# A two-layer graph network on one core: nine gathered slots a tile in place of ten, and three PSUM banks in turn

## The chip, the cores and the metric

The kernel runs on one core of a Trainium2 chip. The metric is the device time of one execution in microseconds (us). The core has five engines with a queue each: TensorE (PE, matrix products; PEld is its loading of weights), VectorE (DVE), ScalarE (ACT), GpSimd (POOL) and SyncE (SP, which issues transfers). Each executes its queue in order; they meet through semaphores. PSUM, into which PE writes, has eight banks of 128 x 512 f32.

## The reference

```
adj: 4096 x 4096, an entry off the diagonal with a chance of 0.00195, values 0.05 to 1; the diagonal always
layer 0:  a = adj + I;  d = rowsum(a) ** -0.5
          out = relu((d a d) @ x @ W.T + b);   h = layernorm(x + out)
layer 1:  the same form, attention of 8 heads over a mask: maximum(adj, I), and -1e16 * (1 - mask) on the scores
          h = layernorm(h + att @ v @ Wo)
```

Entries of `adj` lie below one, so in layer 1 an entry below one off the diagonal still gets a penalty of 1e15 or more; each node attends to itself alone, and the layer comes to one product with `Wv @ Wo`. The kernel tests that this holds (`test`), and has a general kernel behind a branch for the other case. What is left is layer 0, a sparse product: a row of `adj` has 8 edges on average, 21 at most.

## The kernel before

Rows are handled in 32 tiles of 128 (`NT`, `P`). There are two stages with a barrier between.

**First stage.** For each tile, `y = d * (x @ W.T)` is computed and written to DRAM: `x` is loaded, transposed on PE into a PSUM tile `pt` (`transpose_rows`), copied to `xT` by ACT (`evacuate`), multiplied (`times`), scaled by ACT with `d` (`keep_y`) and stored. `d` needs the row's sum, for which the whole tile of `adj` (2 MB) is loaded; ACT sums it (`sum_rows`). On the tiles in `early` and, in the second stage, on the others, DVE extracts the edges: eight segments of 512 columns, in each the eight largest values and their columns (MAX8, FIND_INDEX8), then short steps that sort a row's edges into 24 places of a record `rec` (`extraction`). These are 16 long steps a tile; `some` issues them in portions. Fifteen tiles (`again`) are loaded once more in the second stage (`reload`).

**Matching.** A row with more edges than there are slots passes its surplus to rows with few. `match` takes each tile through six steps: KEY (a key from the number of edges), ACROSS (PE transposes the key into `pk`), RANKS (how many keys are smaller: the row's rank), PERM (DVE compares the rank with `sources` and gets one 0/1 matrix per map), MOVE (PE multiplies the record by these matrices: lane l gets the row of rank l, and in its last slots the surplus of another row), END (DVE reads the moved fields into `wr_all` and `cols_all`). `KH` is 10: ten edges a lane. `ROUTES` has three maps (lane at which rank 0 goes, first and last place of the surplus). `SAME` is the number of slots that only hold a lane's own edges, 5. `pk` and the moved fields lie in one PSUM tile, `bank`; `pt` has two further banks, the sums `acc` five.

**Second stage, the gather loop.** Loop index `i` over the tiles in `order`, inner index `k` over the slots. For each slot POOL issues one indirect transfer of 128 rows of `y` (256 KB, `gather`, 18 slots ahead, 19 buffers), ACT builds the 128 x 128 matrix that puts the lanes' weights into their rows (`spread`: a square and a Relu for the slots from `SAME` on, one scaled copy for the others), and PE adds the product to `zs[i]` (L1265). The last two tiles (`SUMMED`) first add up the `SAME` slots on DVE (`presum`) and have six products (L1084). Behind the tile come `scaled` (L1126), `residual`, the transposes of `h`, the product with `wvo` and the second normalisation, at places that the function `at` sets. The steps of matching have places too:

```
match(*{1: (RANKS,), 3: (MOVE, PERM), 6: (END,), 7: (KEY,), 9: (ACROSS,)}.get(k, ()))
```

The order of instructions on each engine isn't quite that of the program: a planner with its own estimates of durations orders them and gives the PSUM and SBUF buffers, and an instruction waits where a buffer's last reader isn't done. The key's transpose and the first move are kept in program order.

Of the kernel before, what the change touches and what calls it, by code (L numbers as in the profile page):

```python
# [9 lines left out]
FP = mybir.dt.float32  # L10
# [4 lines left out]
P = 128  # L15
# [404 lines left out]
def few_edges_below_one(  # L420
# [18 lines left out]
    nc = tc.nc  # L439
    N, D = x.shape  # L440
    H, _, KD = wks.shape
    NT = N // P
# [7 lines left out]
    TS = SW // P  # L450
    C = SEGS * E
    K = 24
    KH = 10

    ROUTES = ((112, 10, 14), (120, 14, 19), (76, 19, 24))
    SAME = KH - max(hi - lo for _, lo, hi in ROUTES)

    const = ctx.enter_context(tc.tile_pool(name="const", bufs=1))
    small = ctx.enter_context(tc.tile_pool(name="small", bufs=4))
# [3 lines left out]
    keys = ctx.enter_context(tc.tile_pool(name="keys", bufs=2))  # L463
    dram = ctx.enter_context(tc.tile_pool(name="dram", bufs=1, space=bass.MemoryType.DRAM))
    mt = ctx.enter_context(tc.tile_pool(name="match", bufs=1))
    ps_t = ctx.enter_context(tc.tile_pool(name="ps_t", bufs=2, space=bass.MemoryType.PSUM))
    ps_a = ctx.enter_context(tc.tile_pool(name="ps_a", bufs=5, space=bass.MemoryType.PSUM))
    first = ExitStack()
    p1 = first.enter_context(tc.tile_pool(name="first", bufs=2))
# [22 lines left out]

    sources = const.tile([P, 1 + len(ROUTES), P], BF, name="sources")

    def ranks(dst, step, base):
        nc.gpsimd.iota(
            dst, pattern=[[step, dst.shape[1]]], base=base, channel_multiplier=0,
            allow_small_or_imprecise_dtypes=True,
        )

    ranks(sources[:, 0], 2, 1 - P)
    for n, (c, _, _) in enumerate(ROUTES):
        ranks(sources[:, n + 1, : c + 1], -2, 2 * c + 1 - P)
        ranks(sources[:, n + 1, c + 1 :], -2, P - 1)

    place = const.tile([P, 2, C], U32, name="place")
    for f, (per_seg, per_edge, base, shift) in enumerate(
# [16 lines left out]
    own_all = const.tile([P, NT], FP, name="own_all")  # L524
    cols_all = const.tile([P, NT, KH], U32, name="cols_all")

    wr_all = const.tile([P, NT, 4, KH], FP, name="wr_all")
    y = dram.tile([N, D], FP, name="y")
# [20 lines left out]
    order = early + resident + again  # L549
# [110 lines left out]
    def transpose_rows(src, dcs=range(ND)):  # L660
        pt = ps_t.tile([P, 512], FP, name="pt")
        for dc in dcs:
            nc.tensor.transpose(pt[:, ts(dc, P)], src[:, ts(dc, P)], ident)  # L663
        return pt
# [132 lines left out]
        return long, short  # L797


    bank = ps_t.tile([P, 512], FP, name="bank", bufs=1)  # L800
    second = []

    def match_key(t):
# [7 lines left out]
        return key  # L811

    def match_across(key):
        pk = bank[:, :P]
        tc.keep_in_program_order(nc.tensor.transpose(pk, key.to_broadcast([P, P]), ident))  # L815
        return pk

# [17 lines left out]
    def match_move(rec, perm):  # L835

        r = upper(rec)
        merged = bank[:, P : P + 7 * KH].rearrange("p (f k) -> p f k", f=7)
        tc.keep_in_program_order(
            nc.tensor.matmul(merged, perm[:, 0], r[:, :, :KH], start=True, stop=False)  # L840
        )
        for n, (_, lo, hi) in enumerate(ROUTES):
            nc.tensor.matmul(
                merged[:, :, KH - (hi - lo) :], perm[:, n + 1], r[:, :, hi - 1 : lo - 1 : -1],
                start=False, stop=(n == len(ROUTES) - 1),
            )
        return merged
# [15 lines left out]
    matched = set()  # L863
    begun, picked, sorted_ = [], [], []
    KEY, ACROSS, RANKS, PERM, MOVE, END = range(6)
# [73 lines left out]
    queue = list(again)  # L939
    reloaded, scanned = [], []  # L940
# [54 lines left out]
    for t in range(NT + 1):  # L995
# [8 lines left out]
        lo, hi = t + 1 + (t > EARLIER), t + 1 + (t >= EARLIER)  # L1004
        ahead = [j for at, j in due if lo <= at <= hi]
        pts = []
# [42 lines left out]
    SUMMED = (NT - 2, NT - 1)  # L1049
# [20 lines left out]
    def presum(i, k):  # L1070
        g = slots[i * KH]
        w = wr_all[:, order[i], 1, k : k + 1]
        if k == 0:
            nc.scalar.activation(g, g, AF.Copy, scale=w)
            return
        nc.vector.scalar_tensor_tensor(
            g, slots.pop(i * KH + k), w, g, op0=ALU.mult, op1=ALU.add
        )
# [52 lines left out]
    def residual(i, c=slice(0, D), part=0):  # L1131
        if i % 2 == 0 and i not in sts:
            sts[i] = small.tile([P, 2, 5], FP, name="sums")
            sts[i + 1] = sts[i][:, 1]
            pairs[i] = sts[i]
            sts[i] = sts[i][:, 0]
        nc.vector.scalar_tensor_tensor(
            hs[i][:, c], hs[i][:, c], 0.0, xs[i][:, c], op0=ALU.max, op1=ALU.add,
            accum_out=sts[i][:, part : part + 1],
        )  # L1140
# [65 lines left out]
    yo, zs, hs, pts, hTs, ws, sts, pairs, mats, halves = ({} for _ in range(10))  # L1206
# [24 lines left out]
    for i in range(NT + 2):  # L1231
        if i < NT:
            zs[i] = ps_a.tile([P, D], FP, name="acc")
        free = len([t for t in scanned if t in picked])
        p = i - 1
        has_p = 0 <= p < NT
        for k in range(KH):
            ends = p == NT - 1
            t = at("T", i, k)
            if t not in (None, NT - 1):  # L1240
                hTs[t] = evacuate(p2, "hT", transpose_rows(hs[t]))
            t = at("M", i, k)
            if t not in (None, NT - 1):
                ws[t] = times(hTs.pop(t), wvo)
            if i == NT - 1:

                if k <= KH - SAME:
                    summed_products(i, k, HALVES[0])
                if k == 7:
                    scaled(i, HALVES[0])  # L1250
                    residual(i, HALVES[0])
                if k == 8:
                    pts[i] = transpose_rows(hs[i], (0, 1))
                if k == 9:
                    for n in range(KH - SAME + 1):
                        summed_products(i, n, HALVES[1])
                    hTs[i] = p2.tile([P, ND, P], FP, name="hT", bufs=2)
                    nc.scalar.copy(
                        hTs[i][:, 0:2].rearrange("p c s -> p (c s)"), pts[i][:, : 2 * P]
                    )  # L1260
            elif i in SUMMED:
                if k <= KH - SAME:
                    summed_products(i, k)
            elif i < NT:
                nc.tensor.matmul(  # L1265
                    zs[i], mats[i][:, k, :], slots.pop(i * KH + k),
                    start=(k == 0), stop=(k == KH - 1),
                )
            if i < NT:
                gather(i * KH + k + AHEAD)  # L1270
            build(1)
            if i + 1 in SUMMED and k >= 5:
                presum(i + 1, k - 5)
            if k == 1 and has_p and not ends:
                scaled(p)
            some(next(shares, count[1]))
            if k == 1 and has_p and not ends:
                residual(p)
            if ends and k == 0:
                scaled(p, HALVES[1])  # L1280
                residual(p, HALVES[1], 4)
                ws[p] = times(hTs[p], wvo, dcs=(0, 1))
            if ends and k == 2:
                pts[p] = transpose_rows(hs[p], (2, 3))
                nc.scalar.copy(hTs[p][:, 2:].rearrange("p c s -> p (c s)"), pts[p][:, 2 * P : D])
                nc.vector.tensor_tensor(sts[p][:, 0:1], sts[p][:, 0:1], sts[p][:, 4:5], ALU.add)
            if ends and k == 3:
                times(hTs[p], wvo, ws[p], (2, 3))
            if k == 2:
                load_own(i + 2)  # L1290
            if k == 3 and i + 1 < NT:
                own_part(i + 1)
            t = at("Q", i, k)
            if t is not None:
                squares(ws[t], D**-0.5, sts[t][:, 3:4])

            t = at("V", i, k)
            if t is not None:
                variance(t)
                if t >= NT - 2:  # L1300
                    power(t, 1)
                elif t % 2:
                    power(t - 1, 2)
            if k == 6 and i < NT:
                own_bias(i)
            if k == 6 and has_p:
                eps_var(p)
            t = at("F", i, k)
            if t is not None and (t >= NT - 2 or t % 2):
                if t < NT - 2:  # L1310
                    finish(t - 1)
                finish(t)
            if k in (3, 9):
                scan_half()
            if staged[KEY] < NT - 2:
                match(*{1: (RANKS,), 3: (MOVE, PERM), 6: (END,), 7: (KEY,), 9: (ACROSS,)}.get(k, ()))
            elif k % 2:
                match(*ALL)
            if k == 9 and queue and len(reloaded) < free:
                reload()  # L1320
            while k == 1 and i + 2 < NT and order[i + 2] not in matched:
                some(count[0] + 1)
                match(*ALL)
        if i == NT - 7:
            su2 = load_keys()
        if i == NT - 4:
            square_sums(su2)
        if i == NT - 2:
            test()
# [25 lines left out]
```

## Time and profile before

| what | value |
|---|---|
| runs | 746.01, 750.56, 754.48 us; median 750.56 |
| profiled execution | span 744.8 us from first to last instruction; the page has no other time of it |
| PE, DVE, ACT, POOL busy | 591.2, 545.4, 525.2, 393.2 us |
| moved by DMA | 230.54 MB, 310 GB/s over the span |
| first gather | 221.85 us |
| first slot product (L1265) | 228.38 us |
| last output | ACT at 732.91 us |

A row of the page's groups has the line, the engine, the operation, its tiles and how often it stands there; then the busy time, the mean of one in ns, the idle time of the engine just before, and what ended most of it. A row of the timeline has the start and the length in us, and in brackets the idle time before it and who ended it. A program line belongs to the kernel before; the changed kernel's lines are up to nine further down.

### The profile page before, as it was taken

The numbers are of one execution on the slowest core, as the hardware profiler recorded it, in microseconds if no ns is written. First come the engines' busy times: TensorE is split into PE (matmuls) and PEld (weight loads), VectorE is DVE, ScalarE is ACT, GpSimd is POOL, SyncE is SP. The second block draws the span as 40 slices with busy tenths as digits, with TensorE's granted clock in tenths as the row PEclk, the third lists the DMA queues.
The fourth block names the chain that finished last, engine by engine and source line by source line (L and its number), as shares of the span: only waits on it lengthen the run. The fifth ranks groups of instructions, "written<-read, shape, count | busy, mean of one in ns | idle before, by whom it ended". The sixth has DMA issues, their size and how long they took to land. (4 is left out here: it accounts for less than half of the span.)

```text
span 744.8 us, 8023 instructions
## 1 busy us (share of the span) xinstructions
PE 591.2 (79%) x1638; PEld 273.9 (37%) x1638; DVE 545.4 (73%) x2109; ACT 525.2 (71%) x1152; POOL 393.2 (53%) x494
## 2 busy tenths in 40 slices
PE   1799959867815687989979699979996789898692
PEld 0444424433302233434434344434442334343350
DVE  6779899999997289889978799959994443322410
ACT  1787798958975287688958597867884887773432
POOL 3224233322337656766666666666665566667500
PEclk9999999999967778999999899999998899999896
DMA  8999999999947689999999988989996577777601
GB/s 341 403 422 426 425 423 406 421 430 413 423 187 262 198 294 366 343 371 373 380 305 343 325 300 313 337 297 333 351 333 209 171 221 239 224 240 248 199 24 62
DMA packets 54411, 230.54 MB, mean 310 GB/s; under 512 B 8592, under 2 KB 9616, under 8 KB 48080
## 3 DMA queue, kind: packets, MB, share of 16 engines
q0 software_dynamic: 30800, 100.95, 40.6%
q1 hardware_dynamic: 18416, 119.55, 40.5%
q10 hardware_dynamic: 5136, 9.44, 3.4%
q14 instruction: 44, 0.36, 0.1%
q8 instruction: 15, 0.25, 0.1%
HBM read 213.12 MB, written 16.78 MB: 309 GB/s over the span
## 5 line engine op out<-in xcount | busy, mean ns | idle before, releaser
L1057 POOL DMA_INDIRECT g<-y,cols_all x320 | 312.9, 978 | 151.0 <-issue 82.6
L1265 PE MATMUL acc<-g,s_t 128*128 128x512 f32 x600 | 283.6, 619 | 20.0 <-ACT s_t L959 20.0
L731 DVE MAX8 v_all<-a_t 128x8 f32<-128x512 f32 x256 | 168.8, 679 | 18.1 <-DMA a_t<-in_adj_dram 18.1
L732 DVE FIND_INDEX8 idx<-v_all,a_t 128x8 uint32<-128x512 f32 x256 | 174.0, 683 | 0.0
L1265 PEld LDWEIGHTS acc<-g,s_t 128*128 128x128 f32 x600 | 116.2, 200 | 151.9 <-issue 124.4
L675 PE MATMUL acc<-wvo,hT 128*128 128x512 f32 x256 | 125.4, 630 | 25.4 <-issue 14.8
L675 PE MATMUL acc<-wT,xT 128*128 128x512 f32 x256 | 121.7, 621 | 16.4 <-ACT xT L668 12.2
L687 ACT ACTIVATE dump<-a_t 128x2048 uint8<-128x2048 f32 (+1 forms) x52 | 119.5, 2297 | 0.0
L675 PEld LDWEIGHTS acc<-wvo,hT 128*128 128x128 f32 x256 | 49.1, 200 | 87.6 <-issue 71.9
L675 PEld LDWEIGHTS acc<-wT,xT 128*128 128x128 f32 x256 | 48.3, 198 | 72.3 <-issue 50.2
L955 ACT ACTIVATE sq<-cols,wr_all 128x128 f32<-128x128 f32 x192 | 66.9, 391 | 9.9 <-issue 7.3
L959 ACT ACTIVATE s_t<-sq,wr_all 128x128 f32<-128x128 f32 x160 | 72.0, 483 | 1.6 <-ACT sq L955 1.2
L968 ACT ACTIVATE s_t<-s_t,wr_all 128x128 f32<-128x128 f32 x150 | 52.4, 391 | 4.6 <-issue 3.8
L682 ACT ACTIVATE dump<-a_n 128x4096 uint8<-128x4096 f32 x15 | 54.5, 3632 | 0.3 <-DMA a_n<-in_adj_dram 0.3
L744 DVE MAX8 top<-key 128x8 f32<-128x64 f32 x192 | 39.0, 214 | 12.1 <-issue 7.3
L1119 DVE SCALAR_TENSOR_TENSOR yo<-yo,own_all,b_bc 128x512 f32<-128x512 f32 x32 | 23.8, 744 | 24.1 <-DMA yo<-y 10.4
L1126 DVE SCALAR_TENSOR_TENSOR h<-acc,d_all,yo 128x512 f32<-128x512 f32 (+1 forms) x33 | 23.9, 724 | 23.5 <-PE acc L1265 11.3
L540 POOL DMA_DIRECT2D x_t<-in_x_dram x32 | 17.9, 564 | 41.2 <-PE pt L663 41.0
L694 POOL TENSOR_SCALAR deg<-deg_all 128x1 f32<-128x1 f32 x32 | 6.7, 220 | 62.4 <-ACT dump L682 62.3
L704 POOL DMA_DIRECT2D y<-y_t x32 | 19.0, 593 | 38.6 <-ACT y_t L702 38.1
L702 ACT ACTIVATE y_t<-acc,d_all 128x512 f32<-128x512 f32 x32 | 21.6, 686 | 22.6 <-POOL d_all L697 16.7
L815 PE MATMUL bank<-ident,rank_key 128*128 128x128 f32 x32 | 10.2, 320 | 33.4 <-issue 11.5
(123 smaller groups left out, 651.5 us busy)
## 6 DMA issues: line engine op xcount, KB each, us to landing
a_t<-in_adj_dram SPq DMA_DIRECT2D x30, 2048.0 KB
a_n<-in_adj_dram SPq DMA_DIRECT2D x15, 2048.0 KB
x_t<-in_x_dram POOLq DMA_DIRECT2D x32, 256.0 KB
y<-y_t POOLq DMA_DIRECT2D x32, 256.0 KB
yo<-y SPq DMA_DIRECT2D x32, 256.0 KB
x_t<-in_x_dram SPq DMA_DIRECT2D x32, 256.0 KB
out_dram<-r_t ACTq DMA_DIRECT2D x32, 256.0 KB
g<-y,cols_all POOLq DMA_INDIRECT x320
```

Source lines behind the costliest of these rows:

```text
L675: nc.tensor.matmul(u, srcT[:, dc, :], w[:, dc, :], start=(dc == 0), stop=(dc == ND - 1))
L682: nc.scalar.activation(dump[:, : part.shape[1]], part, AF.Copy, accum_out=dst)
L687: nc.scalar.activation(dump[:, o], a_t[:, o], AF.Relu, scale=-1.0, accum_out=neg_all[:, t, halves[0] : halves[0] + 1],)
L731: long.append(lambda o=o, seg=seg: nc.vector.max(v[:, o], seg))
L732: long.append(lambda o=o, seg=seg: nc.vector.max_index(idx[:, o], v[:, o], seg))
L744: return lambda: nc.vector.max(top[:, f, r * 8 : r * 8 + 8], keyf[:, f])
L955: nc.scalar.activation(sq, cols1, AF.Square, bias=wr[:, 2, k : k + 1])
L959: nc.scalar.activation(s_t[:, k, :], away(), AF.Relu, scale=wr[:, 3, k : k + 1], bias=wr[:, 1, k : k + 1],)
L968: nc.scalar.activation(s_t[:, k, :], s_t[:, KH, :], AF.Copy, scale=wr[:, 1, k : k + 1])
L1057: nc.gpsimd.indirect_dma_start(out=slots[j], out_offset=None, in_=y[:, :], in_offset=bass.IndirectOffsetOnAxis(ap=cols_all[:, t, k : k + 1 ...
L1126: nc.vector.scalar_tensor_tensor(hs[i][:, c], zs[i][:, c], d_all[:, order[i] : order[i] + 1], yo[i][:, c], op0=ALU.mult, op1=ALU.add,)
L1265: nc.tensor.matmul(zs[i], mats[i][:, k, :], slots.pop(i * KH + k), start=(k == 0), stop=(k == KH - 1),)
```

## The change

There are nine slots (`KH` 9). The surplus begins at the tenth edge and goes by four maps in place of three. A map is now a list of runs: (lane, width) sends `width` rows, in order of rank, to the lanes that end at `lane`. Lanes in no run get the value 128, which no rank has. The first map moves four places, the others three, so `SAME` stays 5. `bank` is gone: the key and the moved fields each take a tile `pt` like the other transposes, and `ps_t` has three banks in place of two. The places in the loop move with `KH`; since 18 slots ahead are now two whole tiles, the loop that makes sure of a matched tile looks one tile further.

```diff
-    KH = 10
-
-    ROUTES = ((112, 10, 14), (120, 14, 19), (76, 19, 24))
-    SAME = KH - max(hi - lo for _, lo, hi in ROUTES)
+    KH = 9
+
+    ROUTES = (
+        (9, 13, ((127, 21), (102, 3), (96, 2), (93, 8), (84, 1), (82, 2), (79, 13), (63, 1))),
+        (13, 16, ((106, 1), (104, 2), (99, 1), (97, 1), (85, 1), (83, 1), (80, 1), (65, 2),
+                  (62, 2), (58, 1))),
+        (16, 19, ((105, 1), (98, 1), (66, 1), (60, 1))),
+        (19, 22, ((94, 1), (59, 1))),
+    )
+    SAME = KH - max(hi - lo for lo, hi, _ in ROUTES)
...
-    ps_t = ctx.enter_context(tc.tile_pool(name="ps_t", bufs=2, space=bass.MemoryType.PSUM))
+    ps_t = ctx.enter_context(tc.tile_pool(name="ps_t", bufs=3, space=bass.MemoryType.PSUM))
...
+    nc.gpsimd.memset(sources[:, 1:], float(P))
     ranks(sources[:, 0], 2, 1 - P)
-    for n, (c, _, _) in enumerate(ROUTES):
-        ranks(sources[:, n + 1, : c + 1], -2, 2 * c + 1 - P)
-        ranks(sources[:, n + 1, c + 1 :], -2, P - 1)
+    for n, (_, _, runs) in enumerate(ROUTES):
+        r = 0
+        for lane, width in runs:
+            r += width
+            ranks(sources[:, n + 1, lane + 1 - width : lane + 1], -2, 2 * r - 1 - P)
...
-    bank = ps_t.tile([P, 512], FP, name="bank", bufs=1)
...
-        pk = bank[:, :P]
+        pk = ps_t.tile([P, 512], FP, name="pt")[:, :P]
...
-        merged = bank[:, P : P + 7 * KH].rearrange("p (f k) -> p f k", f=7)
+        moved = ps_t.tile([P, 512], FP, name="pt")
+        merged = moved[:, : 7 * KH].rearrange("p (f k) -> p f k", f=7)
...
-                if k == 7:
+                if k == 6:
                     scaled(i, HALVES[0])
                     residual(i, HALVES[0])
+                if k == 7:
+                    pts[i] = transpose_rows(hs[i], (0, 1))
                 if k == 8:
-                    pts[i] = transpose_rows(hs[i], (0, 1))
-                if k == 9:
                     for n in range(KH - SAME + 1):
...
-            if i + 1 in SUMMED and k >= 5:
-                presum(i + 1, k - 5)
+            if i + 1 in SUMMED and k >= KH - SAME:
+                presum(i + 1, k - (KH - SAME))
...
-            if k in (3, 9):
+            if k in (3, KH - 1):
                 scan_half()
             if staged[KEY] < NT - 2:
-                match(*{1: (RANKS,), 3: (MOVE, PERM), 6: (END,), 7: (KEY,), 9: (ACROSS,)}.get(k, ()))
+                match(*{1: (RANKS,), 3: (MOVE, PERM), 6: (END,), 7: (KEY,), KH - 1: (ACROSS,)}.get(k, ()))
...
-            if k == 9 and queue and len(reloaded) < free:
+            if k == KH - 1 and queue and len(reloaded) < free:
                 reload()
-            while k == 1 and i + 2 < NT and order[i + 2] not in matched:
+            while k == KH - 1 and i + 3 < NT and order[i + 3] not in matched:
```

More of the change, by code (lines that the diff above doesn't have):

```diff
@@ L841, in match_move @@
         )
-        for n, (_, lo, hi) in enumerate(ROUTES):
+        for n, (lo, hi, _) in enumerate(ROUTES):
             nc.tensor.matmul(
```

## The prediction

> **What bounds the kernel now.** I read the windows first, because the average shares of the page mix two stages.
>
> ```profile
> 0.00:50.00 50.00, 27.64 (x91) 15.68 (x92) 33.45 (x126) 27.12 (x24) 13.68 (x40) 1.00 0.98 386
> 100.00:150.00 50.00, 38.54 (x125) 18.30 (x123) 49.99 (x225) 43.85 (x41) 17.15 (x37) 0.97 1.01 418
> 300.00:350.00 50.00, 45.34 (x124) 20.41 (x123) 44.28 (x162) 38.19 (x105) 34.56 (x36) 0.97 0.99 359
> 600.00:650.00 50.00, 43.21 (x119) 19.18 (x118) 18.03 (x83) 40.55 (x114) 34.11 (x36) 0.98 0.73 227
> ```
>
> The columns are PE, PEld, DVE, ACT, POOL busy, granted clock, DMA share, GB/s. Up to 221 us (the first stage) DMA and DVE are full and PE is not. From 228 us (the gather loop) PE leads, with DVE close behind until about 560 us and far behind after it.
>
> The timeline of PE gives the loop's pace. The transposes of `h` stand once in each tile: at 299.67 and, 26 tiles on, at 704.20, so 15.56 us a tile; from 284.21 to 554.30 it is 18 tiles of 15.0 us. Three tiles of that timeline:
>
> ```profile
> 440.63 0.60 PE L663 MATMUL pt<-ident,h 128*128 128x128 f32 x4
> 441.07 3.60 PE L1265 MATMUL acc<-g,s_t 128*128 128x512 f32 x8
> 444.50 0.20 PE L840 MATMUL bank<-rec,perm 128*128 128x70 bf16 x1
> 444.54 0.24 PE L843 MATMUL bank<-rec,perm 128*128 128x28 bf16 x3
> 444.62 1.96 PE L1265 MATMUL acc<-g,s_t 128*128 128x512 f32 x4
> 446.42 3.60 PE L675 MATMUL acc<-wvo,hT 128*128 128x512 f32 x8
> 449.85 3.60 PE L1265 MATMUL acc<-g,s_t 128*128 128x512 f32 x8
> 453.29 0.27 PE L815 MATMUL bank<-ident,rank_key 128*128 128x128 f32 x1
> ...
> 330.57 0.47 PE L815 MATMUL bank<-ident,rank_key 128*128 128x128 f32 x1 [2.45 <-DVE wr_all L853]
> ...
> 426.34 0.48 PE L815 MATMUL bank<-ident,rank_key 128*128 128x128 f32 x1 [6.22 <-ACT dump L1145]
> ```
>
> An f32 product is two passes; eight passes start 3.43 us apart (441.07 to 444.50), so one pass costs 0.43 us and one slot's product 0.86 us. A tile is 20 passes for ten slots, 8 for `wvo`, 0.44 for transposes, 0.23 for key and moves: 12.7 us. The tile that begins at 440.63 ends at 453.40 and takes just that. The other tiles lose the rest in waits, and nearly all of them stand in front of the two matching steps that share the one bank: from 300 to 555 us, 15.3 us before L815 and 3.9 us before L840. In the whole loop it is 31.1 us and 9.7 us.
>
> Then the page's groups, for what a slot costs elsewhere:
>
> ```profile
> L1057 POOL DMA_INDIRECT g<-y,cols_all x320 | 312.9, 978 | 151.0 <-issue 82.6
> L1265 PE MATMUL acc<-g,s_t 128*128 128x512 f32 x600 | 283.6, 619 | 20.0 <-ACT s_t L959 20.0
> L955 ACT ACTIVATE sq<-cols,wr_all 128x128 f32<-128x128 f32 x192 | 66.9, 391 | 9.9 <-issue 7.3
> L959 ACT ACTIVATE s_t<-sq,wr_all 128x128 f32<-128x128 f32 x160 | 72.0, 483 | 1.6 <-ACT sq L955 1.2
> ```
>
> Unhindered gathers start 1.25 us apart (221 to 256 us in POOL's timeline, 0.95 busy and 0.30 idle), so ten need 12.5 us of a tile; one `sq` and one `s_t` start 0.68 us apart on ACT.
>
> **The change, part by part.** The profile has a span of 744.8 us and no time of its own; the median of the runs is 750.56, so 5.8 us lie around the span, and I keep them.
>
> *One slot less, PE.* The 600 passes of L1265 become 540: 30 x 0.86 = 25.8 us. The two summed tiles go from six products to five: 0.86 us for the one, 0.86 us for the other, which does it in halves. Together -27.5 us. I take all of it, because PE is the busiest engine of the loop and each other engine is relieved too: POOL by 1.25 us a tile, ACT by 0.68, DMA by 256 KB of some 5.1 MB (345 GB/s x 15.0 us). DVE is not. Its work per tile up to 560 us is 13.2 us (219 us busy between 300 and 550 us, times 15.0). But that is mostly extraction, and in the changed program's order of instructions DVE does six MAX8/FIND_INDEX8 pairs between two L1135 where it does 6.75 now, with the last pairs in tile 23, not 21. The planner has stretched it; 0.75 of a pair with its share of short steps is 1.4 us, so DVE falls to about 11.8 us, beside PE's 11.9 (12.7 less 0.86, and the new map).
>
> *A fourth map.* PE: four moves start within 0.12 us (444.50 to 444.62), so one more is 0.03 us, +1.0 us for 32 tiles. DVE: `perm` goes from 512 to 640 wide. Its median of 345 ns against some 190 ns for the 24-wide steps bounds the growth between 0 and 345/4 = 86 ns; I take 50 ns, and half of it on the path: +0.8 us. END's rows shrink from 10 to 9 columns: nothing.
>
> *Setup on POOL.* 24 iotas and a memset for seven iotas. The seven took 1.10 us, so 17 more and the memset are 2 to 3 us, ahead of the first loads of `x`. These are wanted by PE's transposes at 25.4 us, and POOL is idle from 7.4 to 25.0 us. Zero; without that cover +3.
>
> *Start of the loop.* Until 256 us gathers set the pace, so three tiles gain 1.25 in place of 0.86, and the first product (228.38 us) waits for the builds of its whole tile, one fewer: -1.2 - 0.7 = -1.9 us.
>
> *Three banks, loop.* Before, a key's transpose waits until END has read the moved fields in the same bank, and a move until `above` has read the key. In the new order both still wait for END or `above` in most tiles (the ring of three comes round once per tile), but between move and key PE has nine products to do (7.7 us) where in the first dozen tiles it has four (3.4 us). The 41 us of waits bound this: -41 if all vanish, 0 if they stay as long; above 0 if `h` has to wait as well, some 2 us a tile by the waits seen, so +40. I take -4, near the row of waits that do not depend on the bank (a late DVE makes PE late at `perm` and `h` as well).
>
> *Three banks, first stage.* Twelve transposes of `x` now wait until DVE has read a key or moved fields, where before they waited for ACT only. Behind them in PE's queue stand the products `u`, behind these ACT's `xT` and the row sums that free the loads; from 161 us ACT is idle only 7.5 of 57 us, so what ACT loses late, the stage loses. In the new order PE is two tiles further back when DVE reads the key at its 144th extraction step (150 us), and ACT has three copies of `xT` (0.58 each) more to do. So +2 us. From below 0 (ACT's slack of 7.5 us takes it), from above twelve times the 5.33 us that ACT once waited for a transpose (148.7 us): +56 after the slack.
>
> Sum: -27.5 + 1.0 + 0.8 - 1.9 - 4 + 2 = -29.6: span 715, time **721 us**.
>
> **The clock.** After waits of 4 us and more the first passes are slower: at 385.19, after 4.17 us idle, four passes take 3.67 us in place of 1.88; nine such restarts stand in the loop. The Trainium skill, "TensorE: Matmul & The Clock Gate", section "HAM oscillation — how this bites in real kernels", says that PE's clock halves when it idles longer than some 3.4 us, so that less PE work beside an unchanged partner can cost speed; the 3.67 agrees. By it the sum would be 750 (rival 4), without it 721.
>
> **The rivals.**
> 1. *DVE keeps the pace.* Its extraction is a fixed sum, and up to 560 us it is 88% busy. If it binds, that stretch keeps its length and only the last 9 tiles (0.9 each) and the start gain: -10 + 2, about 742 us. For it: DVE is late at several bank waits. Against it: the thinner order. 18%.
> 2. *Slower: the ring blocks the first stage.* Place: the twelve transposes. Price: 5.33 us each at worst, +56 us, 775 us in all. It decides from eight full waits on (39 us: the slack of 7.5 and the loop's gain of 31.6). For it: DVE is full from 100 to 225 us and PE's queue is in order. Against it: PE's bank waits in that stage cost it 3.9 us in all (before L815 and L840 up to 228 us), since DVE mostly ran ahead. 8%.
> 3. *The bank waits go.* Half of the 41 us more: 702 us. For it: distance 7.7 in place of 3.4 us. Against: END still has to come. 15%.
> 4. *Cold clock.* If PE's idle time gathers into one wait per tile, 1.2 to 1.9 us are lost at each (330.57 and 385.19): 20 tiles take back 30 us, 750 us. It needs that in most tiles; before, nine have it. 5%.
>
> That the change fails to do what it says would mean edges without a slot, and then the general kernel would follow. The matrix has 32,905 edges off the diagonal for 36,864 slots, and the maps place each one; I give it nothing.
>
> **Chances.** The forecast, 712 to 732, has 54%. Below 743.1 (1%, about what this kernel's runs can tell from no change) lie it, rival 3 and two thirds of rival 1: 0.82. Within 1% the rest of 1 and rival 4: 0.10. Slower: 0.08. The range leaves out rivals 2 and 4 and the far end of 3: 702 to 745.
>
> **What would show it.** Right: 288 gathers, 540 passes in the slots' group, quick tiles of 11.8 us, a mean pace near 14.3, the first slot product near 230 us. Wrong: a first product past 240 us (rival 2), extraction that ends at 555 us again with DVE above 90% (1), waits before L823 and L849 under 15 us (3), granted clock below 0.9 between 300 and 550 us (4).

## The result

On the chip of the first measurement the changed kernel takes 705.13 us (median of 702.33 to 709.10) and the kernel before 751.27 us (746.01 to 754.48): a ratio of 0.939, with a 95% interval of 0.933 to 0.945. That is 46 us less, where 30 were forecast: 705.13 us lies below the 712 to 732 that the prediction gave the most weight, and inside its range of 702 to 745. The profiled execution of the changed kernel has a span of 705.5 us and a time of 707.32 us; the two profiled spans differ by 39.3 us.

**The profile after.** The same four windows, in the same columns (PE, PEld, DVE, ACT, POOL busy, granted clock, DMA share, GB/s):

```profile
0.00:50.00 50.00, 29.37 (x100) 16.90 (x101) 33.00 (x124) 28.20 (x26) 15.26 (x59) 1.00 0.98 385
100.00:150.00 50.00, 38.14 (x128) 18.14 (x126) 49.68 (x219) 37.68 (x36) 15.86 (x33) 0.93 1.01 419
300.00:350.00 50.00, 45.39 (x133) 20.71 (x132) 45.68 (x171) 42.15 (x111) 32.72 (x35) 0.97 0.97 369
600.00:650.00 50.00, 46.31 (x130) 21.03 (x129) 14.85 (x56) 34.99 (x101) 32.66 (x34) 0.93 0.71 228
```

They look as they did: the loop still has PE in front and POOL at some 33 of 50 us. A tile without a wait, in PE's timeline of the changed kernel:

```profile
537.66 0.60 PE L672 MATMUL pt<-ident,h 128*128 128x128 f32 x4
538.10 3.60 PE L1274 MATMUL acc<-g,s_t 128*128 128x512 f32 x8
541.53 0.20 PE L849 MATMUL pt<-rec,perm 128*128 128x63 bf16 x1
541.57 0.27 PE L852 MATMUL pt<-rec,perm 128*128 128x28 bf16 x4
541.68 1.96 PE L1274 MATMUL acc<-g,s_t 128*128 128x512 f32 x4
543.48 3.60 PE L684 MATMUL acc<-wvo,hT 128*128 128x512 f32 x8
546.91 2.74 PE L1274 MATMUL acc<-g,s_t 128*128 128x512 f32 x6
549.49 0.60 PE L672 MATMUL pt<-ident,h 128*128 128x128 f32 x4
```

From 537.66 to 549.49 it is 11.83 us, against 12.77 before. But the mean tile fell by more: 26 tiles from 299.65 to 661.11 are 13.90 us each, against 15.56, so 1.66 us a tile where PE's own work fell by 0.9. The groups of the page:

```profile
L1066 POOL DMA_INDIRECT g<-y,cols_all x288 | 281.8, 978 | 129.0 <-issue 73.2 <-PE acc L1274 24.4 <-remote 11.3
L1274 PE MATMUL acc<-g,s_t 128*128 128x512 f32 x540 | 261.7, 624 | 30.9 <-ACT s_t L977 21.9 <-DMA g<-y,cols_all 4.6 <-issue 4.2
...
L964 ACT ACTIVATE sq<-cols,wr_all 128x128 f32<-128x128 f32 x160 | 57.3, 393 | 3.3 <-DMA y<-y_t 2.4 <-ACT r_t L1179 0.5 <-issue 0.3
L968 ACT ACTIVATE s_t<-sq,wr_all 128x128 f32<-128x128 f32 x128 | 56.8, 484 | 2.7 <-remote 2.5
```

32 gathers and 60 passes fewer, as forecast. The waits of PE before the key's transpose and the first move fell from 40.8 to 16.3 us in the loop, which looked at first like the other half of the gain. The experiments, all on other chips, say otherwise.

### The profile page after: what moved, and what is told of

It reads as the page before. It is cut to its first block, busy times and chain, and to the rows that moved or that the text cites. A ratio compares the mean times of both kernels' runs of the same rounds, so it can differ in the third digit from the quotient of the medians.

```text
span 705.5 us, 7873 instructions
## 1 busy us (share of the span) xinstructions
PE 569.9 (81%) x1604; PEld 262.8 (37%) x1604; DVE 543.3 (77%) x2109; ACT 504.9 (72%) x1088; POOL 364.3 (52%) x481
## 5 line engine op out<-in xcount | busy, mean ns | idle before, releaser
L1066 POOL DMA_INDIRECT g<-y,cols_all x288 | 281.8, 978 | 129.0 <-issue 73.2
L1274 PE MATMUL acc<-g,s_t 128*128 128x512 f32 x540 | 261.7, 624 | 30.9 <-ACT s_t L977 21.9
L1274 PEld LDWEIGHTS acc<-g,s_t 128*128 128x128 f32 x540 | 102.1, 199 | 146.7 <-issue 114.7
L684 PE MATMUL acc<-wT,xT 128*128 128x512 f32 x256 | 123.2, 632 | 26.2 <-ACT xT L677 25.5
L964 ACT ACTIVATE sq<-cols,wr_all 128x128 f32<-128x128 f32 x160 | 57.3, 393 | 3.3 <-DMA y<-y_t 2.4
L968 ACT ACTIVATE s_t<-sq,wr_all 128x128 f32<-128x128 f32 x128 | 56.8, 484 | 2.7 <-remote 2.5
L977 ACT ACTIVATE s_t<-s_t,wr_all 128x128 f32<-128x128 f32 x150 | 48.5, 388 | 2.0 <-ACT dump L1154 1.5
L1173 POOL TENSOR_TENSOR sums<-sums,mhalf 128x2 f32<-128x2 f32 (+1 forms) x17 | 12.6, 740 | 48.7 <-DVE sums L1165 46.2
L677 ACT COPY hT<-pt 128x512 f32<-128x512 f32 x31 | 17.8, 574 | 26.4 <-PE acc L1274 14.9
L1154 ACT ACTIVATE dump<-acc 128x512 f32<-128x512 f32 x32 | 18.6, 583 | 24.1 <-PE acc L684 12.3
L865 ACT ACTIVATE wr_all<-wr_all 128x9 f32<-128x9 f32 x24 | 5.0, 207 | 41.6 <-DVE wr_all L860 13.1
```

The source lines that it names most:

```text
L684: nc.tensor.matmul(u, srcT[:, dc, :], w[:, dc, :], start=(dc == 0), stop=(dc == ND - 1))
L964: nc.scalar.activation(sq, cols1, AF.Square, bias=wr[:, 2, k : k + 1])
L968: nc.scalar.activation(s_t[:, k, :], away(), AF.Relu, scale=wr[:, 3, k : k + 1], bias=wr[:, 1, k : k + 1],)
L977: nc.scalar.activation(s_t[:, k, :], s_t[:, KH, :], AF.Copy, scale=wr[:, 1, k : k + 1])
L1066: nc.gpsimd.indirect_dma_start(out=slots[j], out_offset=None, in_=y[:, :], in_offset=bass.IndirectOffsetOnAxis(ap=cols_all[:, t, k : k + 1 ...
L1274: nc.tensor.matmul(zs[i], mats[i][:, k, :], slots.pop(i * KH + k), start=(k == 0), stop=(k == KH - 1),)
```

## The experiments

They fell on two other chips. There the kernel before takes 708 to 710 us and the changed one 661 (on one of the two), so ratios to the kernel before on the same chip are compared. A trace shows a single execution, which lies up to 6 us from the median of its kernel.

**Banks alone, slots alone.** The kernel before with the three banks only:

```diff
-    bank = ps_t.tile([P, 512], FP, name="bank", bufs=1)      # ps_t: bufs 2 -> 3
-        pk = bank[:, :P]
+        pk = ps_t.tile([P, 512], FP, name="pt")[:, :P]
-        merged = bank[:, P : P + 7 * KH].rearrange("p (f k) -> p f k", f=7)
+        moved = ps_t.tile([P, 512], FP, name="pt")
+        merged = moved[:, : 7 * KH].rearrange("p (f k) -> p f k", f=7)
```

> The kernel before, with ten slots and three maps, but with the key's transpose and the moved fields taking turns with the transposes in three banks. Theory A (slots and banks are two gains that add up; the banks are worth some 20 us in the loop, because the key is no longer transposed a few products behind the move that it waits for, and cost some 5 us in the first stage): 751 + 5 - 20 = 736 us (730 to 742); waits of PE before the key's transpose and before the moves in the loop fall from 40.8 us to about 20; the first slot product is near 233 us. Theory B (the gain beyond the slots comes from the thinner work per tile, not from the banks): 751 to 756 us, with the waits at 35 us or more. My prediction's terms for this part were -4 and +2: 749 us.

Measured: 713.48 us, ratio 1.004 (1.0005 to 1.007). In its loop PE waits 1.7 us before the key's transpose and not at all before the moves, and that gained nothing. The theory that the banks give half of the gain fell.

The reverse is the changed kernel with these lines undone, nine slots and one shared bank:

> The changed kernel with nine slots and four maps, but with the one shared bank of before for key and moved fields. Theory A: only the slots' gain remains, 27.5 us less 1.8 for the map and with 1.9 at the start: 751 - 27.6 = 723 us (718 to 729); the first slot product is near 228 us, and the waits before the key's transpose and the moves stay near 40 us. Theory B: 700 to 708 us, with those waits near 18 us as in the changed kernel.

Measured: 657.38 us, ratio 0.927 (0.923 to 0.931). The slots alone give the whole gain and more, nearly twice PE's 27.5 us. PE waits only 3.5 us before the key's transpose and the first move in this loop, with the shared bank, where theory A of the expectation had 40; and the first slot product comes at 232.24 us, not near 228. So the forecast had the wrong engine's price for a slot, or there is a second one.

**The kernels themselves on such a chip.**

> The kernel before unaltered, for its trace. If the 40.8 us of waits before the key's transpose and the moves come from the shared bank, they stand here as well. If they come from what held DVE up on the first chip, they are under 10 us on a chip where this kernel takes 709 us.

> The changed kernel unaltered, beside its variants. The first group of runs fell on a chip on which the kernel before took 709.4 us and not 751. If the ratio of the change belongs to the kernel, it is 0.939 here too (666 us against 709). If the three banks cost their 5 us in the first stage on that chip and give nothing back in the loop, the ratio is 0.93 to 0.935 (660 to 663), against 0.927 for nine slots with the shared bank.

Measured: the changed kernel 660.61 us, ratio 0.932 (0.925 to 0.939), as the second guess had it. The kernel before has 2.2 us of waits before the key's transpose here:

```profile
L815 PE MATMUL bank<-ident,rank_key 128*128 128x128 f32 x23 | 6.5, 283 | 2.2 <-ACT rank_key L808 2.2
```

With 10.4 us before the first move it has 12.6 us, not 40.8, so most of what the prediction counted belonged to that one chip (last section). The banks alone were not run there: what the 24.5 us of waits that went there were worth is not shown.

**One price of the slot at a time.** Two variants give one engine its tenth slot back. First PE, the slot's product done twice:

```diff
+                if k == 0:
+                    nc.tensor.matmul(zs[i], mats[i][:, 0, :], slots[i * KH], start=True, stop=True)
                 nc.tensor.matmul(zs[i], mats[i][:, k, :], slots.pop(i * KH + k), ...
```

> The changed kernel with the first slot's product done twice in 30 tiles: PE has 60 more passes of L1274, all other engines their work of nine slots. If PE's passes set the loop's pace, the prediction's price holds: 30 x 0.86 = +25.8 us. If the loop's pace is set by gathers, DVE or ACT, it is under +8 us.

Then POOL and the transfers, a gather that nobody reads:

```diff
+        if k == 0:
+            nc.gpsimd.indirect_dma_start(
+                out=p2.tile([P, D], FP, name="spare", bufs=1), out_offset=None, in_=y[:, :],
+                in_offset=bass.IndirectOffsetOnAxis(ap=cols_all[:, t, 1:2], axis=0))
```

A line not shown here gives `sq` two buffers in place of three, to make room.

> The changed kernel with one more gather in each tile, into a spare tile that nobody reads (sq has two buffers and not three, to make room): POOL has 32 x 1.25 us and the DMA queues 32 x 256 KB more. If PE's passes set the pace, 0 to +4 us. If the transfers do (256 KB at some 350 GB/s are 0.75 us), +20 to +24 us; if POOL's issue does, +35 to +40 us.

Measured: the product back 688.07 us (0.970, 0.963 to 0.978), +27.5 us; the gather back 710.92 us (1.004, 1.0005 to 1.008), +50.3 us. **The gather alone takes back the whole gain**, though PE has nine products. The 50 us lie above the 35 to 40 expected for POOL's issue. Some of that is the experiment's own: the spare tile has one buffer, and POOL waited 8.6 us for it. The buffer that `sq` lost shows nowhere: ACT is idle before `sq` for 0.4 us of the loop in both kernels. The two profiled executions differ by 45.3 us, 42.8 of them between the first and the last gather.

The reason stands in POOL's timeline. In the kernel before (its trace on this kind of chip):

```profile
426.72 0.94 POOL L1057 DMA_INDIRECT g<-y,cols_all  x1 [0.30 <-issue]
427.97 0.94 POOL L1057 DMA_INDIRECT g<-y,cols_all  x1 [0.30 <-PE acc L1265]
428.93 0.83 POOL L1164 TENSOR_TENSOR sums<-sums,mhalf 128x2 f32<-128x2 f32 x1
429.93 1.00 POOL L1057 DMA_INDIRECT g<-y,cols_all  x1 [0.18 <-issue]
431.24 0.96 POOL L1057 DMA_INDIRECT g<-y,cols_all  x1 [0.31 <-issue]
```

A gather behind a gather starts 0.30 us after the end of the first, whatever the label, and no row counts that time as busy. So POOL at 38 of 50 us is a full POOL. The kernel before is there from 550 us on, and so is the variant with the gather back (two windows of each):

```profile
550.00:600.00 50.00, 44.25 (x119) 20.12 (x118) 20.71 (x95) 43.75 (x125) 38.64 (x41) 0.93 0.80 256
600.00:650.00 50.00, 50.00 (x146) 23.05 (x145) 14.73 (x50) 37.37 (x107) 38.66 (x41) 1.00 0.84 261
550.00:600.00 50.00, 47.44 (x137) 21.42 (x136) 39.40 (x148) 45.47 (x128) 38.65 (x41) 1.00 0.84 267
600.00:650.00 50.00, 43.92 (x125) 19.96 (x124) 14.92 (x58) 35.50 (x103) 38.63 (x41) 0.93 0.82 255
```

41 instructions of 0.95 + 0.30 us are 51 us, in 50, while DMA is at 0.80 to 0.84. From 250 to 550 us the kernel before has 36 to 39 of them in 50 us, 45 to 49 us, and the rest is waits. With its mean of 0.98 us busy a gather costs POOL 1.28 us, and a tile of ten costs 10 x 1.28 + 0.36 (half of a power, which moves the next gather back by 0.71 us: 427.97 to 429.93 is 1.96 and not 1.25) = 13.2 us; a tile of nine 11.9. PE's quick tiles are 12.8 and 11.9 us. So by these sums **POOL was the longest engine of the loop** before, by a little, and after, the two are level. What to set against it is the stretch from the first to the last gather, which each trace gives in one row (the last two numbers before the form):

```profile
L1057 POOL DMA_INDIRECT g<-y,cols_all x320: 940/948/1450, 223.4 to 668.2; - x160
```

```profile
L1066 POOL DMA_INDIRECT g<-y,cols_all x288: 942/951/1497, 226.8 to 624.5; - x144
```

```profile
L1066 POOL DMA_INDIRECT g<-y,cols_all x288: 942/948/1586, 229.8 to 651.5; - x144
```

```profile
L1066 POOL DMA_INDIRECT g<-y,cols_all x288: 940/948/1453, 226.4 to 666.9; - x144
```

These are before, after, product back and gather back (whose other 32 gathers stand in a row of their own). In us:

| kernel | products, gathers a tile | PE, 32 quick tiles | POOL, 32 tiles | stretch | more than the longer |
|---|---|---|---|---|---|
| before | 10, 10 | 410 | 421 | 445 | 24 |
| gather back | 9, 10 | 381 | 421 | 441 | 20 |
| product back | 10, 9 | 410 | 380 | 422 | 12 |
| after | 9, 9 | 381 | 380 | 398 | 17 |

The stretch is the longer of the two sums and 12 to 24 us; it is 22 us more with the banks alone (227.6 to 670.5) and 14 with the slots alone (225.3 to 620.6). Because PE's sum is close behind POOL's, the two prices don't add: by the table one gather less is worth 23 us (before against product back), one product less 4 (before against gather back), and both together 47.

The pair on the first chip fits as a difference: from 221.8 to 704.0 us before and from 227.5 to 664.7 us after, 45.0 us less, where 32 x 1.28 = 41 would be the gathers; 5.7 us are lost at the start, and the 40.8 us behind the last gather are the same: -39.3, the difference of the two spans. But there the stretches are 61 and 56 us longer than the longer sum, so that POOL set the pace on that chip too is argued, not shown. The Trainium skill, "Perfetto Trace Analysis", section "What "DMA-bound" means", has this case: a kernel can be bound on the queue that issues its DMAs, whose profiled window is the making of descriptors and not the transfer. It looks for a track that is solid with slices; here the track of a full POOL shows gaps of 0.30 us.

What stays open is the part of the transfers before 550 us, where the variant's DMA share is 0.85 to 1.00 and POOL is near full too. At some 360 GB/s, 256 KB take 0.73 us; 32 of them are 23 us and alone don't make 41. No run gives back the issue without its transfer. The table also leaves out DVE, which is full in the changed kernel on this kind of chip from 400 to 550 us:

```profile
400.00:450.00 50.00, 49.74 (x147) 23.12 (x146) 50.00 (x190) 44.13 (x124) 36.85 (x38) 1.00 0.99 361
450.00:500.00 50.00, 49.05 (x142) 22.29 (x141) 50.00 (x194) 45.52 (x127) 36.73 (x38) 1.00 0.99 368
```

DVE has the same number of instructions in the four kernels, so it doesn't explain their differences; but in these 150 us the changed kernel has PE and DVE full, POOL close to it and DMA at 0.89 to 0.99, so no single one of them sets the pace there.

**A third candidate: r_t behind the gathers.** One long wait in the changed kernel's trace on this kind of chip, on ACT and then on PE:

```profile
310.08 1.27 ACT L1179 ACTIVATE r_t<-acc,sums 128x512 f32<-128x512 f32 x2 [14.49 <-POOL sums L1173]
...
314.29 5.33 PE L684 MATMUL acc<-wvo,hT 128*128 128x512 f32 x8 [8.69 <-ACT hT L677]
```

POOL's small power stands in its queue behind the gathers, ACT's `r_t` waits for it, `hT` is behind `r_t` on ACT, and PE waits for `hT`. If this were how a gather becomes dear, a later `r_t` would make it cheap:

```diff
-        far = {"T": (2, 0), "M": (2, 6), "Q": (3, 1), "V": (3, 4), "F": (3, 8)}
+        far = {"T": (2, 0), "M": (2, 6), "Q": (3, 1), "V": (3, 4), "F": (4, 4)}
```

> The changed kernel with r_t and its store five slots later (place (4, 4) and not (3, 8)); no work is removed. Theory C: POOL's small power of sums stands in its queue behind the gathers; ACT's r_t waits for it (46.2 us in the changed kernel's trace), the copy hT stands behind r_t on ACT, and PE waits for hT before the product with wvo (21.3 us in that trace, and slower first passes after each long wait). Then ACT's waits before r_t fall below 15 us, PE's before wvo below 10 us, and the time is 0.905 to 0.92 of the kernel before (643 to 653 us where that takes 710). Rival: the waits move to another place (a PSUM bank held longer by r_t, or a gather): 0.93 to 0.94.

> The changed kernel with one more gather in each tile into a spare tile, as before, and r_t five slots later. With r_t in its old place the extra gather cost 50 us (0.932 to 1.004 of the kernel before). Theory C: most of that came by way of POOL's power and r_t (86.1 us of waits before r_t); without it POOL's 320 issues of 1.25 us from 227 us on end near 627 us, and the kernel takes 0.935 to 0.965 (664 to 685 us of 710). Rival: the gather itself (issue, transfer) is the price, wherever r_t stands: 0.99 to 1.005.

> The kernel before, ten slots and shared bank, with r_t and its store at place (4, 4) and not (3, 8). Theory C: its trace on this kind of chip has 57.1 us of ACT waiting for POOL's power before r_t and 22.2 us of PE waiting for hT; most of the latter goes: 0.96 to 0.98 (682 to 696 us of 710). Then what the change gains over the kernel before, beyond PE's 27.5 us, is that chain. Rival: within 0.99 to 1.005.

Measured: the changed kernel with `r_t` later 657.64 us, 0.928 (0.923 to 0.933), between the two bands expected; with the gather back 712.58 us, 1.006 (1.002 to 1.009); the kernel before 703.58 us, 0.993 (0.990 to 0.996). Theory C fell: PE's wait for `hT` went from 21.3 to 9.2 us as it said, and the gather was as dear as ever. ACT's waits before `r_t` hardly moved, first in the changed kernel, then with `r_t` later:

```profile
ACT r_t L1179 <- POOL sums L1173: 46.2, 11, 14.5
```

```profile
ACT r_t L1179 <- POOL sums L1173: 37.5, 11, 8.3
```

`r_t` still waits for POOL in its new place, as it must if POOL sets the pace. What is gained, 5 us in the kernel before and 3 us in the changed one (the latter within the intervals), stands in the traces as the excess over the longer sum, which falls from 24 to 12 us and from 17 to 10; the 12 comes from an execution 6 us below the median of its kernel.

**The first stage.** The matching steps keep a bank to themselves until the loop begins, and only there do the three take turns:

```diff
+    def next_bank(matching):
+        if second:
+            turn[0] += 1
+            matching = turn[0] % 3 == 0
+        return (ps_t.tile([P, 512], FP, name="bank", bufs=1) if matching
+                else ps_t.tile([P, 512], FP, name="pt"))
```

> The changed kernel, but in the first stage the transposes of x have two banks and the matching steps the third, as before; the three banks take turns only in the gather loop. Theory A (the changed kernel's first slot product comes 5 us later, at 233.55 against 228.38 us, because transposes of x wait for DVE's reads): first slot product at 228 to 230 us, total 705 - 5 = 700 us (697 to 703). Rival (the delay has another cause, such as DVE's own order or the wider perm): first slot product at 233 us again and 705 us.

Measured: 657.94 us, ratio 0.927 (0.923 to 0.930). The first slot product comes at 228.03 us, the first gather at 221.5 and not 226.8. POOL's waits before the loads of `x`, changed kernel and this one:

```profile
POOL x_t L549 <- PE pt L672: 66.8, 19, 13.0
```

```profile
POOL x_t L549 <- PE pt L672: 42.8, 14, 5.8
```

The last variant below has the same first stage and its first gather at 223.7 us. So a delay of 3 to 5 us by the ring in the first stage is shown; that it comes out in the total fits the numbers (0.005 less than the changed kernel), but the intervals overlap. Banks alone against the kernel before, changed kernel against slots alone: both pairs say that the three banks cost some 3 to 4 us, the first just clear of its interval, the second not.

**Two more maps**, which select no lane:

```diff
         (19, 22, ((94, 1), (59, 1))),
+        (19, 22, ()),
+        (19, 22, ()),
```

> The changed kernel with two further maps that select no lane (six in all): two more small bf16 moves per tile on PE, and perm grows from 640 to 896 wide on DVE. By the prediction's price for one map (+1.0 on PE and +0.8 on DVE) two cost +3.6 us: 708.7 us. Rival 1 (a map is hidden): within 1 us of 705. Rival 2 (each move takes its row's 185 ns on PE and nothing overlaps): 2 x 0.185 x 32 = +12 us, 717 us. The mean of perm on DVE should rise by 100 ns by the size taken, by 172 ns if it goes with its width.

Measured: 659.89 us, ratio 0.930 (0.927 to 0.934), no difference from the changed kernel that can be told. `perm` on DVE means 365 ns at 512 wide, 376 at 640 and 442 at 896: so 11 to 33 ns for a map.

**Two together**, the bank apart in the first stage and `r_t` later:

> The changed kernel with two parts together: in the first stage the transposes of x have two banks and the matching steps the third, and r_t stands five slots later. If both gains add, 3 to 4 us below r_t later alone: 0.90 to 0.915 of the kernel before. If the first stage's gain is lost in the loop's waits, the same as r_t later alone.

Measured: 654.35 us, ratio 0.921 (0.917 to 0.926), the shortest of all and below both kernels. It is 3.3 us below `r_t` later alone, as expected if both gains add, though the intervals overlap; the ratio falls short of the 0.90 to 0.915 expected.

## Why the prediction was right, and where it was not

- **One slot less, -27.5 us: the term that was mis-sized.** The prediction took the price of a slot from PE, as the busiest engine, and noted POOL's ten gathers at 12.5 us a tile beside PE's 12.7. It used the shortest spacing (0.95 + 0.30) and left out the power in the same queue. With the mean and the power POOL needs 13.2 us. The slot was then worth 1.28 us a tile, 41 us in all; in the runs the gather put back cost 43 us between the first and the last gather. The sign was right because a slot relieves every engine; the price of PE was right for PE, and putting the product back cost 27.5 us, near the 25.8 worked out. That the wrong engine's price still landed in the range is luck: with 12.5 us for POOL beside 12.7 for PE the prediction had two tiles that are nearly equal, and did not ask what a small error in either would do to the price.
- **Three banks in the loop, -4 us.** In the runs the stretch of the gathers is 445 us in the kernel before and 443 with the banks alone (227.6 to 670.5 us), so about -2. Rival 3 (702 us; half of 41 off 721 is 701) came near the measured time. On the other chips its cause was not there: the bank waits went and nothing was gained. On the first chip they did fall by more than half, to 16.3 us, where its mark was 15; whether that gained anything there is not shown.
- **Three banks in the first stage, +2 us.** Right in kind, and too small: 3 to 5 us, by the bank apart. In the first pair PE's waits for `xT` rose from 12.2 to 25.5 us in that stage. Rival 2 (blocked first stage, 775 us) was this mechanism at eleven times its size; the first product came at 233.55 us, under the mark of 240.
- **Start of the loop, -1.9 us.** Not seen by itself: the first product was forecast near 230 us, the ring's delay covers the gain of one build, and the gathers' part is in the 41.
- **A fourth map, +1.8 us.** On the high side: two more cost nothing measurable, and the mean of `perm` grew by 28 ns on the first chip and 11 on another, where 50 were taken.
- **Setup on POOL, 0.** Nothing speaks against it: in the runs with the bank apart or shared the first gather comes at 221.5 and 225.3 us, with all 24 iotas in them.
- **DVE.** Rival 1 (742 us) did not come, though its mark was half met: DVE is 96% busy from 450 to 550 us. The 555 us in that mark was a misreading: the last FIND_INDEX8 starts at 577.9 us in the kernel before, and at 573.3 in the changed one. What spoke against the rival held on the first chip: the same extraction lies over more tiles, and 18 of them (299.65 to 549.49 us) take 13.9 us each, not 15.0. On the other chips DVE is full for 150 us of the changed kernel's loop (above), so the rival had named a real limit, though not the price.
- **The clock.** Granted 0.90 to 1.00 from 300 to 550 us, not below 0.9, so rival 4 (750 us) did not come. Restarts are still there: in PE's timeline of the first trace of the changed kernel eight passes take 6.49 us after a wait, and 3.60 without one (543.48):

```profile
586.11 6.49 PE L684 MATMUL acc<-wvo,hT 128*128 128x512 f32 x8 [4.97 <-ACT hT L677]
```

- **The sum.** Forecast for the span were -29.6 us, measured -39.3: 41 by the gathers, if POOL's price holds on that chip, and 4.0 left over in their stretch, less 5.7 at the start. That this 4.0 equals the -4 for the banks is chance: the runs show some 2 us for these. The 9.7 us between are 13.5 too few for the slot and 1.8 for a map whose cost can't be measured, less 1.9 for the start of the loop and 3.7 for the first stage. The other 6 of the 16 us by which 721 was high are no part of the change: 5.8 us were kept around the span where the profiled execution has 1.8, and it lies 2.2 us above its median. (The chances below 743.1 us add to 0.81, not 0.82.)

## What to carry to other kernels

Before a saving is priced by the busiest engine, work out what each engine needs for one turn of the loop, spacing included: POOL, issuing these gathers, is full at a busy share of some 76% (0.95 of 1.25 us), and everything else in its queue adds to it. When two engines need almost the same, the gain of removing work from both goes by the longer one, before and after, and giving each its work back in turn shows which it is. Waits that vanish elsewhere were worth little here, however many microseconds the profile listed for them: 11 us of bank waits about 2 us, 12 us of waits for `hT` about 3.

## What was not expected of the hardware

- The same kernel took 751 us on the first chip and 708 to 710 on the others, the changed one 705 and 661, at almost the same ratio (0.939 and 0.932). Durations of single instructions agree (a gather 978 and 976 ns, FIND_INDEX8 683 and 684). On the first chip DVE stands idle in front of steps that depend on its own earlier ones. In the timeline of DVE in the first trace of the kernel before:

```profile
250.75 0.23 DVE L744 MAX8 top<-key 128x8 f32<-128x64 f32 x1 [3.42 <-issue]
...
258.45 0.23 DVE L744 MAX8 top<-key 128x8 f32<-128x64 f32 x1 [3.89 <-issue]
```

  In the traces of the other chips DVE waits 0.5 us or less in all before these steps in the loop. The first chip's traces also hold about half as many semaphore records (9,671 against 20,193 for the kernel before), so the releasers that they name are less to be trusted. What held DVE up there is not settled. The gathers' stretch is 37 us longer there before and 39 us longer after, so their difference is nearly the same (45.0 and 47.1 us).
- In the kernel with the gather back, 320 gathers and 540 passes take as long as 320 and 600: 60 passes of PE less for nothing, behind a queue whose busy share reads 56% of the span.
